# Second-layer attention scores: three bf16 terms in three passes, or two float32r terms in one

## The chip, the cores and the metric

The kernel runs on one core of one Trainium2 chip, in one launch. The metric is the device time of that launch in microseconds. A profiled execution of the same program gives a span and the instructions of each engine: PE (TensorE matmul), PEld (its weight loads), ACT (ScalarE), DVE (VectorE), POOL (GpSimd) and SP (SyncE, which issues most DMAs).

## What is computed

The input x has shape (4, 64, 64, 128): four images of 4096 tokens with 128 channels. Layer 0 is a gated residual block with two 3x3 convolutions and masked single-head attention. Layer 1 is full attention with 16 heads of 8 channels, a gated feed-forward block, and a mixture of 8 experts of which each token uses two. The change concerns the attention of layer 1. Cut to that, the reference is

```python
q = (x @ wq).reshape(bsz, seqlen, N_HEADS, HEAD_DIM)
k = (x @ wk).reshape(bsz, seqlen, N_HEADS, HEAD_DIM)
v = (x @ wv).reshape(bsz, seqlen, N_HEADS, HEAD_DIM)
scores = jnp.einsum('bqhd,bkhd->bhqk', q, k)
probs = jax.nn.softmax(scores.astype(jnp.float32), axis=-1).astype(q.dtype)
attn = jnp.einsum('bhqk,bkhd->bqhd', probs, v).reshape(bsz, seqlen, DIM)
```

Everything is in float32. For each image and head this is a 4096 x 4096 matrix of scores, so 268 million exponentials per image and 1074 million in all.

## The kernel before

The four images (batches) are worked one after the other. For each, the program runs layer 0's convolutions (L245 to L307), layer 0's attention (L309 to L427), layer 1's attention (`l1_attention`, L430 to L564), the feed-forward block and the experts. A tile framework turns the program into one instruction stream per engine. It works out which instruction must wait for which from the tiles and slices that they read and write, and it may put an instruction of a later part between earlier ones when those are not ready.

**Exact scores from short numbers.** Queries and keys are float32. To multiply them on bf16 paths without loss, `three_terms` (L234) splits each number into three bf16 terms: ScalarE rounds the first, VectorE subtracts it, GpSimd rounds the second, VectorE subtracts again. This is done for 8 chunks of 512 tokens per image (L435 to L445), and the terms are stored in DRAM tensors `d_k` and `d_q`.

**Layout.** Four heads make a group (`NG1` = 4 groups), each in its own slot of 32 rows (partitions). `keys(g)` (L469) loads a group's keys: 8 channels x 3 key terms = 24 rows per head, all 4096 tokens, in bf16. Two buffers hold this group's keys and the next one's. `queries(g, c)` (L477) loads 512 queries with each of their three terms repeated over the three key terms. A score needs all nine products of terms; the 24 rows give the products of three key terms with one query term, and three matmuls that accumulate in PSUM add up the three query terms.

**Order of the work.** A block is one group with one chunk of 512 queries: 32 blocks per image, 128 in all. In each block the loop at L541 runs over 32 key tiles of 128 keys. One such step is

```python
            for kt in range(NT):
                ss = [s_tile(), s_tile()]
                for i in range(NTERM):
                    for j in range(NSLOT):
...
                late.append((n, kt, es))
                if len(late) > LAG:
                    finish(*late.pop(0))
```

that is, 12 score matmuls (L546) in three passes over four slots, into two PSUM tiles of 128 x 1024 (two heads each, two banks each), then two exponentials on ScalarE (L556) from PSUM to SBUF, then the value matmuls (`add_up`, L507 and L509) of the step two steps back (`LAG` = 2). Those are plain float32, one per head, each with its own 32 output columns of the array, and they accumulate values and row sums in `acc` over the block. There are three PSUM score tiles, so a score matmul must wait until the exponential three tiles back has read its tile. At a block's end VectorE copies `acc` to SBUF (L524); the next block's first value matmuls must wait for that. One step later, four transposes (L495) and two VectorE instructions (L498, L500) turn the block's result into rows by token.

SP's queue carries, in this order, the chunk stores (L444, L445), the loads of queries (L483, four per block, one block ahead) and the loads of keys (L474, four per group, a group ahead).

Of the kernel before, what the change touches and what calls it, by code (L numbers as in the profile page):

```python
# [8 lines left out]

FP = mybir.dt.float32  # L10
BF = mybir.dt.bfloat16
AF = mybir.ActivationFunctionType
ALU = mybir.AluOpType
AX = mybir.AxisListType

P = 128
C = 128
IMG = 64
N = IMG * IMG
NT = N // P  # L20
QB = 512
NQ = N // QB
# [4 lines left out]
SLOT = 32  # L27
NSLOT = P // SLOT
# [3 lines left out]
NH1, HD1 = 16, 8  # L32
NG1 = NH1 // NSLOT
HIDDEN = 344
FCH = [(0, 128), (128, 128), (256, 88)]
NE = 8

NTERM = 3  # L40
# [49 lines left out]
def fast_path(ctx: ExitStack, tc: tile.TileContext, a: dict, where: dict, out: bass.AP, verdict):  # L90

    nc = tc.nc
    x = a["x"]
    B = x.shape[0]
    LAG = 2

    const = ctx.enter_context(tc.tile_pool(name="f_const", bufs=1))
    big = ctx.enter_context(tc.tile_pool(name="f_big", bufs=1))
    ep = ctx.enter_context(tc.tile_pool(name="f_ep", bufs=8))
    wk = ctx.enter_context(tc.tile_pool(name="f_wk", bufs=2))  # L100
    sm = ctx.enter_context(tc.tile_pool(name="f_sm", bufs=2))
    dram = ctx.enter_context(tc.tile_pool(name="f_dram", bufs=2, space=bass.MemoryType.DRAM))
    ps_s = ctx.enter_context(tc.tile_pool(name="f_ps_s", bufs=3, space=bass.MemoryType.PSUM))
    ps_o = ctx.enter_context(tc.tile_pool(name="f_ps_o", bufs=1, space=bass.MemoryType.PSUM))
    ps_m = ctx.enter_context(tc.tile_pool(name="f_ps_m", bufs=1, space=bass.MemoryType.PSUM))

    def s_tile():
        return ps_s.tile([P, 1024], FP, tag="s", name="s")

    def m_tile():  # L110
        return ps_m.tile([P, QB], FP, tag="m", name="m")
# [1 line left out]
    def e_tile():  # L113
        return ep.tile([P, 1024], FP, tag="e", name="e")
# [119 lines left out]
    def three_terms(src):  # L234

        xs = wk.tile([P, NTERM, 1024], BF, tag="x", name="x")
        rest = e_tile()
        nc.scalar.copy(xs[:, 0, :], src)
        nc.vector.tensor_tensor(rest, src, xs[:, 0, :], ALU.subtract)
        nc.gpsimd.tensor_copy(xs[:, 1, :], rest)  # L240
        nc.vector.tensor_tensor(xs[:, 2, :], rest, xs[:, 1, :], ALU.subtract)
        return xs
# [186 lines left out]

    def l1_attention(b, yT, h):  # L430

        d_k = dram.tile([P, NTERM, N], BF, tag="k1", name="d_k1")
        d_q = dram.tile([NQ, P, NTERM, QB], BF, tag="q1", name="d_q1")
        top = sm.tile([P, 2, NQ], FP, tag="top", name="top")
        for c in range(NQ):  # L435
            cols = slice(c * QB, (c + 1) * QB)
            ps = s_tile()
            nc.tensor.matmul(ps[:, :QB], lhsT=wq1, rhs=yT[:, cols], start=True, stop=True)
            nc.tensor.matmul(ps[:, QB:], lhsT=wk1, rhs=yT[:, cols], start=True, stop=True)
            nc.vector.tensor_reduce(  # L440
                top[:, :, c], ps.rearrange("p (j n) -> p j n", j=2), AX.X, ALU.max, apply_absolute_value=True
            )
            terms = three_terms(ps)
            nc.sync.dma_start(out=d_k[:, :, cols], in_=terms[:, :, QB:])  # L444
            nc.sync.dma_start(out=d_q[c], in_=terms[:, :, :QB])  # L445

        tops = sm.tile([P, 2], FP, tag="tops", name="tops")
        nc.vector.tensor_reduce(tops, top, AX.X, ALU.max)
        nc.vector.tensor_tensor(seen[:, 2, b : b + 1], tops[:, 0:1], tops[:, 1:2], ALU.mult)
        nc.vector.tensor_scalar(seen[:, 2, b : b + 1], seen[:, 2, b : b + 1], 1e30, None, ALU.min)  # L450

        top_v = sm.tile([P, NT // 8], FP, tag="topv", name="topv")
        for s in range(NT // 8):
            ps = s_tile()
            for k in range(8):
                i = 8 * s + k
                nc.tensor.matmul(
                    ps[:, k * P : (k + 1) * P], lhsT=yT[:, i * P : (i + 1) * P], rhs=wv1, start=True, stop=True
                )
            nc.vector.tensor_copy(  # L460
                v1[:, 8 * s : 8 * s + 8, :, 1:], ps.rearrange("p (k h d) -> p k h d", h=NH1, d=HD1)
            )
            nc.vector.tensor_reduce(top_v[:, s : s + 1], ps, AX.X, ALU.max, apply_absolute_value=True)
        nc.vector.tensor_reduce(seen[:, 3, b : b + 1], top_v, AX.X, ALU.max)


        rows = HD1 * NTERM

        def keys(g):  # L469
            kx = big.tile([P, N], BF, tag="kx", bufs=2, name="kx")  # L470
            for j in range(NSLOT):
                head = NSLOT * g + j
                src = d_k[head * HD1 : (head + 1) * HD1].rearrange("d y n -> (d y) n")
                nc.sync.dma_start(out=kx[j * SLOT : j * SLOT + rows, :], in_=src)  # L474
            return kx

        def queries(g, c):  # L477

            qx = wk.tile([P, NTERM, QB], BF, tag="qx", name="qx")
            for j in range(NSLOT):  # L480
                head = NSLOT * g + j
                src = d_q[c][head * HD1 : (head + 1) * HD1].rearrange("d x n -> d (x n)")
                nc.sync.dma_start(  # L483
                    out=qx[j * SLOT : j * SLOT + rows].rearrange("p x n -> p (x n)"),
                    in_=src.unsqueeze(1).to_broadcast([HD1, NTERM, NTERM * QB]),
                )
            return qx

        nt = big.tile([P, NT, C], FP, tag="y", name="nt")

        def by_token(g, c, at):

            ps = m_tile()
            for k in range(4):
                nc.tensor.transpose(ps[:, k * P : (k + 1) * P], at[:, k * P : (k + 1) * P], ident)  # L495
            pj = ps.rearrange("p (k j s) -> p k j s", j=NSLOT, s=SLOT)
            rc = sm.tile([P, 4, NSLOT], FP, tag="rc", name="rc")
            nc.vector.reciprocal(rc, pj[:, :, :, 0])  # L498
            gc = slice(g * NSLOT * HD1, (g + 1) * NSLOT * HD1)
            nc.vector.tensor_tensor(  # L500
                nt[:, 4 * c : 4 * c + 4, gc].rearrange("p k (j d) -> p k j d", d=HD1),
                pj[:, :, :, 1 : 1 + HD1],
                rc.unsqueeze(3).to_broadcast([P, 4, NSLOT, HD1]),
                ALU.mult,
            )

        def add_up(g, c, kt, es):  # L507
            for j in range(NSLOT):
                nc.tensor.matmul(  # L509
                    acc[j * SLOT : j * SLOT + 1 + HD1, :],  # L510
                    lhsT=v1[:, kt, NSLOT * g + j, :],
                    rhs=es[j // 2][:, (j % 2) * QB : (j % 2 + 1) * QB],
                    start=kt == 0,
                    stop=kt == NT - 1,
                )

        order = [(g, c) for g in range(NG1) for c in range(NQ)]
        ready = []

        def finish(n, kt, es):  # L520
            add_up(*order[n], kt, es)
            if kt == NT - 1:
                at = wk.tile([P, QB], FP, tag="at", name="at1")
                nc.vector.tensor_copy(at, acc)  # L524
                ready.append(at)
            if kt == 1 and ready:
                by_token(*order[n - 1], ready.pop())

        kx, qx = keys(0), queries(0, 0)
        kx_next = qx_next = None  # L530
        late = []
        for n, (g, c) in enumerate(order):
            if n:
                qx = qx_next
                if c == 0:
                    kx = kx_next
            if n + 1 < len(order):
                qx_next = queries(*order[n + 1])
            if c == 0 and g + 1 < NG1:
                kx_next = keys(g + 1)  # L540
            for kt in range(NT):  # L541
                ss = [s_tile(), s_tile()]
                for i in range(NTERM):
                    for j in range(NSLOT):
                        r = slice(j * SLOT, j * SLOT + rows)
                        nc.tensor.matmul(  # L546
                            ss[j // 2][:, (j % 2) * QB : (j % 2 + 1) * QB],
                            lhsT=kx[r, kt * P : (kt + 1) * P],
                            rhs=qx[r, i, :],
                            start=i == 0,  # L550
                            stop=i == NTERM - 1,
                        )
                es = []
                for ps in ss:
                    e = e_tile()
                    nc.scalar.activation(e, ps, AF.Exp)  # L556
                    es.append(e)
                late.append((n, kt, es))
                if len(late) > LAG:
                    finish(*late.pop(0))  # L560
        for item in late:
            finish(*item)
        by_token(*order[-1], ready.pop())
        return nt  # L564

# [847 lines left out]
```

## Time and profile before

| what | value |
|---|---|
| time, median of 3 runs | 10427.56 us (10423.74 to 10437.85) |
| time of the profiled execution | 10433.93 us |
| its span | 10432.1 us |
| mean granted TensorE clock | 0.966 |
| exponentials of layer 1 (L556) | 8192 |
| score matmuls (L546) | 49,152 records, median 374 ns |
| value matmuls (L509) | 32,768 records, median 597 ns |
| first and last exponential of layer 1's attention, image 0 | starts 419.6 us, next image's starts 3023.0 us |

A busy time is the time in which at least one instruction of an engine was under way. Matmuls overlap: a record of 374 ns does not mean that the next one starts 374 ns later. So a busy PE is not a PE at its peak, and the same holds for ACT, whose instructions overlap by about a tenth. To see what paces a loop one needs the distance from start to start, and what an engine was waiting for in the gaps. A profile row of a group gives line, engine, operation, output and inputs, shapes and count; then busy time and mean length of one (ns), and after the bar the idle time before them with what ended it.

### The profile page before, as it was taken

Reading aid. Unit: us, or ns where it says so; the run is one execution under the profiler, and the core shown is the slowest. Engines: PE = TensorE matmul, PEld = TensorE weight load, DVE = VectorE, ACT = ScalarE, POOL = GpSimd, SP = SyncE. Lnnn points to the kernel's source line nnn. Section 1 sums busy time; section 2 is a strip of 40 time slices with the busy share of each in tenths; the row PEclk is TensorE's granted clock in tenths of the full one; section 3 lists DMA queues with packets and bytes.
Section 4 is the critical chain, followed back from the end, with each engine's and each line's share of the span. In section 5 each row is a group of like instructions: output and inputs, shape, how many; then the busy total and the mean of one; then the engine's idle time right before and its main releaser. Section 6 shows DMA issues by size and latency. Waiting matters only on the chain.

```text
span 10432.1 us, 204188 instructions
## 1 busy us (share of the span) xinstructions
PE 9972.6 (96%) x90561; PEld 3179.9 (30%) x90565; DVE 1150.2 (11%) x3539; ACT 8198.4 (79%) x8965; POOL 184.3 (2%) x177
## 2 busy tenths in 40 slices
PE   8899999997989999999798999999979899999997
PEld 4322222224432222222442222222244222222224
DVE  1200000004220000000412000000051200000005
ACT  1699999991169999999116999999911799999991
POOL 0000000000000000000000000000000000000000
PEclk9999999998999999999889999999988999999998
DMA  1100000000010000000001000000000100000000
GB/s 26 35 6 10 6 9 7 6 5 15 5 34 6 10 6 9 7 6 5 16 4 35 7 9 6 10 6 6 5 16 4 35 7 9 6 10 6 6 5 9
DMA packets 86914, 112.51 MB, mean 11 GB/s; under 512 B 8835, under 2 KB 71779, under 8 KB 84195
## 3 DMA queue, kind: packets, MB, share of 16 engines
q1 hardware_dynamic: 83267, 97.59, 3.2%
q8 instruction: 710, 11.63, 0.5%
q10 hardware_dynamic: 2752, 1.77, 0.1%
q14 instruction: 185, 1.52, 0.0%
HBM read 64.99 MB, written 34.34 MB: 10 GB/s over the span
## 4 chain that ended last, share of the span: by engine, by line
PE 93%; DVE 4%; DMA 1%; ACT 1%; issue 0%; SPq 0%; POOL 0%; DVEq 0%; ACTq 0%; POOLq 0%
PE acc L509 38%; PE s L546 35%; PE s L291 5%; PE s L276 2%; PE s L666 2%; PE acc L381 2%; DVE t L675 2%; PE s L402 1%; PE s L583 1%; PE s L584 1%; PE m L495 1%; PE m L592 1%; PE m L231 1%; PE s L367 1%; PE m L574 0%
## 5 line engine op out<-in xcount | busy, mean ns | idle before, releaser
L556 ACT ACTIVATE e<-s 128x1024 f32<-128x1024 f32 x8192 | 7642.7, 1022 | 149.5 <-PE s L546 149.5
L509 PE MATMUL acc<-e,f_v 128*9 128x512 f32 x32768 | 4296.2, 595 | 4.5 <-ACT e L556 4.5
L546 PE MATMUL s<-qx,kx 24*128 24x512 bf16 x49152 | 3926.0, 377 | 29.5 <-DMA kx<-d_k 28.5
L546 PEld LDWEIGHTS <-kx 24*128 24x128 bf16 x49152 | 1548.0, 91 | 3823.5 <-issue 3467.2
L509 PEld LDWEIGHTS acc<-e,f_v 128*9 128x9 f32 x32768 | 486.7, 88 | 1753.4 <-issue 1687.1
L524 DVE COPY at<-acc 128x512 f32<-128x512 f32 x128 | 88.6, 692 | 7149.6 <-PE acc L509 7149.6
L291 PE MATMUL s<-c,f_w2c 128*128 128x512 f32 x1152 | 499.9, 592 | 0.0
L666 PE MATMUL s<-f_we,e 128*128 128x512 f32 x512 | 313.1, 763 | 58.2 <-DVE t L675 53.2
L299 ACT ACTIVATE e<-s,f_b 128x512 f32<-128x512 f32 x32 | 22.0, 687 | 422.8 <-PE s L291 422.7
L675 DVE SCALAR_TENSOR_TENSOR t<-s,gate,t 128x128 f32<-128x128 f32 x1024 | 305.9, 343 | 5.3 <-PE s L666 2.5
L291 PEld LDWEIGHTS s<-c,f_w2c 128*128 128x128 f32 x1152 | 215.5, 189 | 263.5 <-issue 263.5
L418 ACT ACTIVATE e<-s 128x1024 f32<-128x1024 f32 x224 | 217.6, 1021 | 91.1 <-PE s L402 90.4
L276 PE MATMUL s<-e,f_w1c 128*128 128x512 f32 x576 | 249.9, 596 | 3.1 <-DVE t L675 1.9
L402 PE MATMUL s<-qk 36*128 36x512 bf16 (+1 forms) x576 | 169.3, 388 | 76.0 <-DMA qk<-d_q 74.1
L655 ACT COPY g<-m 8x512 f32<-8x512 f32 x32 | 18.4, 575 | 230.4 <-PE m L653 230.4
L232 ACT COPY e<-m 128x512 f32<-128x512 f32 x64 | 37.5, 586 | 204.4 <-PE m L231 204.4
L381 PE MATMUL acc<-e,f_v 128*17 128x512 f32 (+3 forms) x1152 | 197.7, 600 | 0.0
L586 ACT ACTIVATE e<-s 128x512 f32<-128x512 f32 (+1 forms) x96 | 56.8, 596 | 165.6 <-PE s L584 165.5
L588 POOL TENSOR_TENSOR t<-t,h 128x512 f32<-128x512 f32 x32 | 40.5, 1266 | 8117.7 <-DVE h L577 8117.7
L666 PEld LDWEIGHTS s<-f_we,e 128*128 128x128 f32 x512 | 118.7, 247 | 202.9 <-issue 120.9
L283 ACT ACTIVATE c<-s,f_b 128x1024 f32<-128x1024 f32 x16 | 17.9, 1118 | 186.7 <-PE s L276 186.7
L276 PEld LDWEIGHTS s<-e,f_w1c 128*128 128x128 f32 x576 | 109.2, 190 | 141.7 <-issue 141.0
(146 smaller groups left out, 2962.0 us busy)
## 6 DMA issues: line engine op xcount, KB each, us to landing
qx<-d_q SPq DMA_DIRECT2D x512, 72.0 KB
d_k<-x SPq DMA_DIRECT2D x32, 384.0 KB
d_q<-x SPq DMA_DIRECT2D x32, 384.0 KB
kx<-d_k SPq DMA_DIRECT2D x64, 192.0 KB
t<-in_x_dram SPq DMA_DIRECT2D x16, 512.0 KB
out_dram<-t SPq DMA_DIRECT2D x32, 256.0 KB
f_w2c<-in_L_conv_W_dram ACTq DMA_DIRECT2D x1, 1152.0 KB
qk<-d_q SPq DMA_DIRECT2D x12, 96.0 KB
```

The costliest lines, as they stand in the source:

```text
L231: nc.tensor.transpose(ps[:, k * P : (k + 1) * P], src[:, k, :], ident)
L276: nc.tensor.matmul(rows(ps[:, h * QB : (h + 1) * QB]), lhsT=w1c[:, tap, :], rhs=e0[:, r0 : r0 + 8, kx : kx + IMG], start=(tap == 0), stop= ...
L291: nc.tensor.matmul(rows(ps[:, h * QB : (h + 1) * QB]), lhsT=w2c[:, tap, h * C : (h + 1) * C], rhs=c1[:, 8 * c + ky : 8 * c + ky + 8, kx : ...
L367: nc.tensor.matmul(ps[:, k * C : (k + 1) * C], lhsT=l_, rhs=w3f, start=True, stop=True)
L381: nc.tensor.matmul(acc[j * SLOT : j * SLOT + 1 + DV0, off:], lhsT=v0[:, kt, :], rhs=e[:, lo:hi], start=r == 0, stop=r == c,)
L402: nc.tensor.matmul(ps[:, lo:hi], lhsT=kx[:kr, kt * P : (kt + 1) * P], rhs=qx[:kr, c * QB + off : (c + 1) * QB], start=True, stop=r < c,)
L418: nc.scalar.activation(e, ps, AF.Exp)
L509: nc.tensor.matmul(acc[j * SLOT : j * SLOT + 1 + HD1, :], lhsT=v1[:, kt, NSLOT * g + j, :], rhs=es[j // 2][:, (j % 2) * QB : (j % 2 + 1) * ...
L546: nc.tensor.matmul(ss[j // 2][:, (j % 2) * QB : (j % 2 + 1) * QB], lhsT=kx[r, kt * P : (kt + 1) * P], rhs=qx[r, i, :], start=i == 0, stop= ...
L556: nc.scalar.activation(e, ps, AF.Exp)
L666: nc.tensor.matmul(px[:, h * QB : (h + 1) * QB], lhsT=yT[:, k * P : (k + 1) * P], rhs=we_f[:, h * QB : (h + 1) * QB], start=True, stop=True,)
L675: nc.vector.scalar_tensor_tensor(tk, px[:, n * C : (n + 1) * C], gate[:, k, n : n + 1], tk, ALU.mult, ALU.add)
```

## The change

Queries and keys of layer 1 are split into two terms of the type float32r (a rounded form of float32) instead of three of bf16. ScalarE writes the rounded first term, VectorE the remainder; GpSimd and the second subtraction are no longer used here. The terms take 4 bytes each. All four products of terms fit into a head's slot (8 channels x 2 x 2 = 32 rows), so one matmul per head replaces three. The queries are stored twice in DRAM, in the layout in which they are loaded, so a block's queries are one load. The keys have one buffer instead of two; a group's keys are loaded in four quarters of 1024 tokens, after the last scores of the group before. The three PSUM score tiles become slices of one tile of six banks. The loop runs over tiles of two heads; `LAG` = 2 counts such tiles, so the value matmuls of a step come after the scores of the next step. What L524 and L495 do is unchanged.

```diff
-            terms = three_terms(ps)
+            terms = wk.tile([P, 2, 1024], FP, tag="x", name="two")
+            nc.scalar.copy(terms[:, 0, :].bitcast(FR), ps)
+            nc.vector.tensor_tensor(terms[:, 1, :].bitcast(FR), ps, terms[:, 0, :], ALU.subtract)
             nc.sync.dma_start(out=d_k[:, :, cols], in_=terms[:, :, QB:])
-            nc.sync.dma_start(out=d_q[c], in_=terms[:, :, :QB])
+            for y in range(2):
+                nc.sync.dma_start(out=d_q[c][:, y], in_=terms[:, :, :QB])
...
+        kx = big.tile([P, N], FP, tag="kx", bufs=1, name="kx")
         def keys(g):
-            kx = big.tile([P, N], BF, tag="kx", bufs=2, name="kx")
-            for j in range(NSLOT):
...
+            src = d_k[g * SLOT : (g + 1) * SLOT].rearrange("d y n -> (d y) n")
+            for s in range(4):
+                cols = slice(s * N // 4, (s + 1) * N // 4)
+                nc.sync.dma_start(
+                    out=kx[:, cols], in_=src[:, cols].unsqueeze(1).to_broadcast([2 * SLOT, 2, N // 4])
+                )
...
+        work = [(n, kt, j) for n in range(len(order)) for kt in range(NT) for j in range(NSLOT)]
...
+        for first in range(0, len(work), WIDE):
+            now = work[first : first + WIDE]
+            ps = s_tile(WIDE)
+            for i, (n, kt, j) in enumerate(now):
...
+                r = slice(j * SLOT, (j + 1) * SLOT)
+                nc.tensor.matmul(
+                    ps[:, i * QB : (i + 1) * QB],
+                    lhsT=kx[r, kt * P : (kt + 1) * P].bitcast(FR),
+                    rhs=qx[r, :].bitcast(FR),
+                    start=True,
+                    stop=True,
+                )
+                g, c = order[n]
+                if c == NQ - 1 and kt == NT - 1 and j == NSLOT - 1 and g + 1 < NG1:
+                    keys(g + 1)
+            e = ep.tile([P, WIDE * QB], FP, tag="e", name="e")
+            nc.scalar.activation(e[:, : len(now) * QB], ps[:, : len(now) * QB], AF.Exp)
+            late.append([(w, e[:, i * QB : (i + 1) * QB]) for i, w in enumerate(now)])
+            if len(late) > LAG:
+                late_now = late.pop(0)
...
+            for (n, kt, j), part in late_now:
+                have[j] = part
+                if j == NSLOT - 1:
+                    add_up(n, kt, have)
```

More of the change, by code (lines that the diff above doesn't have):

```diff
@@ L11 @@
 BF = mybir.dt.bfloat16
+FR = mybir.dt.float32r
 AF = mybir.ActivationFunctionType
@@ L95, in fast_path @@
     LAG = 2
+    WIDE = 2
     const = ctx.enter_context(tc.tile_pool(name="f_const", bufs=1))
@@ L102, in fast_path, with s_tile @@
     dram = ctx.enter_context(tc.tile_pool(name="f_dram", bufs=2, space=bass.MemoryType.DRAM))
-    ps_s = ctx.enter_context(tc.tile_pool(name="f_ps_s", bufs=3, space=bass.MemoryType.PSUM))
+    ps_s = ctx.enter_context(tc.tile_pool(name="f_ps_s", bufs=1, space=bass.MemoryType.PSUM))
     ps_o = ctx.enter_context(tc.tile_pool(name="f_ps_o", bufs=1, space=bass.MemoryType.PSUM))
     ps_m = ctx.enter_context(tc.tile_pool(name="f_ps_m", bufs=1, space=bass.MemoryType.PSUM))
-    def s_tile():
-        return ps_s.tile([P, 1024], FP, tag="s", name="s")
+    banks = ps_s.tile([P, 6, QB], FP, tag="s", name="s")
+    turn = [0]
+    def s_tile(n=2):
+        at = turn[0] if turn[0] + n <= 6 else 0
+        turn[0] = at + n
+        return banks[:, at : at + n, :].rearrange("p b n -> p (b n)")
     def m_tile():
@@ L430, in l1_attention @@
     def l1_attention(b, yT, h):
-        d_k = dram.tile([P, NTERM, N], BF, tag="k1", name="d_k1")
-        d_q = dram.tile([NQ, P, NTERM, QB], BF, tag="q1", name="d_q1")
+        d_k = dram.tile([P, 2, N], FP, tag="k1", name="d_k1")
+        d_q = dram.tile([NQ, P, 2, 2, QB], FP, tag="q1", name="d_q1")
         top = sm.tile([P, 2, NQ], FP, tag="top", name="top")
@@ L464, in l1_attention @@
         nc.vector.tensor_reduce(seen[:, 3, b : b + 1], top_v, AX.X, ALU.max)
-        rows = HD1 * NTERM
+        kx = big.tile([P, N], FP, tag="kx", bufs=1, name="kx")
         def keys(g):
-            kx = big.tile([P, N], BF, tag="kx", bufs=2, name="kx")
-            for j in range(NSLOT):
[L472 to L475, printed above, removed]
-        def queries(g, c):
[L479 to L486, printed above, removed]
+            src = d_k[g * SLOT : (g + 1) * SLOT].rearrange("d y n -> (d y) n")
[4 more added lines that the diff above has]
+                )
+        def queries(g, c):
+            qx = wk.tile([P, QB], FP, tag="qx", name="qx")
+            nc.sync.dma_start(out=qx, in_=d_q[c][g * SLOT : (g + 1) * SLOT].rearrange("d y x n -> (d y x) n"))
             return qx
@@ L505, in by_token, with add_up @@
             )
-        def add_up(g, c, kt, es):
+        order = [(g, c) for g in range(NG1) for c in range(NQ)]
+        ready = []
+        def add_up(n, kt, es):
+            g, c = order[n]
             for j in range(NSLOT):
@@ L511, in add_up @@
                     lhsT=v1[:, kt, NSLOT * g + j, :],
-                    rhs=es[j // 2][:, (j % 2) * QB : (j % 2 + 1) * QB],
+                    rhs=es[j],
                     start=kt == 0,
@@ L515, in add_up @@
                 )
[L517 to L521, printed above, removed]
             if kt == NT - 1:
@@ L527, in finish @@
                 by_token(*order[n - 1], ready.pop())
[L529 to L560, printed above, removed]
@@ L561, in l1_attention @@
-        for item in late:
-            finish(*item)
+        work = [(n, kt, j) for n in range(len(order)) for kt in range(NT) for j in range(NSLOT)]
+        late, qx, qx_next = [], None, queries(0, 0)
+        have = {}
+        keys(0)
+        for first in range(0, len(work), WIDE):
+            now = work[first : first + WIDE]
+            ps = s_tile(WIDE)
+            for i, (n, kt, j) in enumerate(now):
+                if kt == 0 and j == 0:
+                    qx = qx_next
+                    if n + 1 < len(order):
+                        qx_next = queries(*order[n + 1])
+                r = slice(j * SLOT, (j + 1) * SLOT)
[6 more added lines that the diff above has]
+                )
+                g, c = order[n]
+                if c == NQ - 1 and kt == NT - 1 and j == NSLOT - 1 and g + 1 < NG1:
[5 more added lines that the diff above has]
+                late_now = late.pop(0)
+            else:
+                late_now = []
+            if first + WIDE >= len(work):
+                late_now += [w for ws in late for w in ws]
+            for (n, kt, j), part in late_now:
+                have[j] = part
+                if j == NSLOT - 1:
+                    add_up(n, kt, have)
```

## The prediction, made before the result was known

> **What bounds the kernel now.** I read the page's busy shares first, then its costliest groups.
>
> ```profile
> PE 9972.6 (96%) x90561; PEld 3179.9 (30%) x90565; DVE 1150.2 (11%) x3539; ACT 8198.4 (79%) x8965; POOL 184.3 (2%) x177
> ...
> PE 93%; DVE 4%; DMA 1%; ACT 1%; issue 0%; SPq 0%; POOL 0%; DVEq 0%; ACTq 0%; POOLq 0%
> ...
> L556 ACT ACTIVATE e<-s 128x1024 f32<-128x1024 f32 x8192 | 7642.7, 1022 | 149.5 <-PE s L546 149.5
> L509 PE MATMUL acc<-e,f_v 128*9 128x512 f32 x32768 | 4296.2, 595 | 4.5 <-ACT e L556 4.5
> L546 PE MATMUL s<-qx,kx 24*128 24x512 bf16 x49152 | 3926.0, 377 | 29.5 <-DMA kx<-d_k 28.5
> ```
>
> The chain that ended last gives PE 93%, which reads as "PE-bound, so a third of the score matmuls is worth 2/3 of 3926 us". The L556 row forbids that: in the same stretch ACT is busy 7642.7 us and waited for PE only 149.5 us. The two engines run nose to tail. The timeline of a piece of second-layer attention shows how (start, length, engine, line, count):
>
> ```profile
> 698.56 7.56 ACT L556 ACTIVATE e<-s 128x1024 f32<-128x1024 f32 x8
> ...
> 700.39 1.04 PE L509 MATMUL acc<-e,f_v 128*9 128x512 f32 x8
> ...
> 701.37 0.99 PE L546 MATMUL s<-qx,kx 24*128 24x512 bf16 x12
> ```
>
> A step (one key tile, four heads) is 12 score matmuls, 8 records of value matmuls and two exponentials. Eight exponentials in 7.56 us start (7.56-1.02)/7 = 0.934 us apart. The question is how much of that is ACT's own pace. The next lines are ACT alone over two blocks (a block is 32 steps), then the same place over 1.9 us, then PE there:
>
> ```profile
> 1035.65 59.70 ACT L556 ACTIVATE e<-s 128x1024 f32<-128x1024 f32 x64 [0.51 <-PE s L546]
> 1095.87 59.70 ACT L556 ACTIVATE e<-s 128x1024 f32<-128x1024 f32 x64 [0.51 <-PE s L546]
> ```
> ```profile
> 1035.65 2.85 ACT L556 ACTIVATE e<-s 128x1024 f32<-128x1024 f32 x3 [0.51 <-PE s L546]
> ```
> ```profile
> 1031.30 0.12 PEld L509 LDWEIGHTS acc<-e,f_v 128*9 128x9 f32 x8 [0.46 <-DVE at L524]
> ...
> 1033.17 1.05 PE L509 MATMUL acc<-e,f_v 128*9 128x512 f32 x8
> ...
> 1034.14 0.65 PE L495 MATMUL m<-f_consts,at 128*128 128x128 f32 x4
> ...
> 1034.73 0.83 PE L546 MATMUL s<-qx,kx 24*128 24x512 bf16 x12
> ...
> 1035.49 1.05 PE L509 MATMUL acc<-e,f_v 128*9 128x512 f32 x8
> ```
>
> Right after a stall, where scores lie ready, three exponentials start (2.85-1.02)/2 = 0.915 us apart; 0.92 is common elsewhere. I take 0.917 as ACT's floor. A block now lasts 1095.87-1035.65 = 60.22 us. At the floor it would last 64 x 0.917 = 58.69. So of 60.22, only 1.53 us can be won while 64 exponentials remain: 0.9 from steps in which ACT waits a little, 0.6 from one stall of 0.51 us behind the four transposes of L495 (value matmuls to scores take 1034.73-1033.17 = 1.56 there, 0.98 elsewhere). **ACT is the bound that the change cannot move**: 8192 exponentials of 1024 columns stay.
>
> **The change, part by part.**
>
> *Scores.* Per step, 12 bf16 matmuls in three accumulating passes become 4 float32r matmuls in one. Before, three passes without a wait take 1035.49-1034.73 = 0.75 us until the value matmuls; a pass is (0.83-0.37)/2 = 0.23 (0.37 is one matmul's record), so one pass leaves 0.75-0.46 = 0.29. PE's step is then 0.98+0.29 = 1.27 us of ACT's 1.83: PE ceases to pace. No row shows float32r. Lower bound: the bf16 pass, 0.23. Upper bound: plain fp32, where the chain lists 36 records of L291 (18 matmuls) in 15.46 us, 0.86 each, 0.63 more than bf16. I take the bf16 end: L509's 16,384 calls make 32,768 records, so fp32 runs as two records each, which a number already rounded to the short type has no need of. Weight loads: 91 ns now, 140 (L495) to 189 (L291) for 128 f32 columns; 0 to 0.1 us more per step.
>
> The Trainium skill, "TensorE: Matmul & The Clock Gate", section "Weight-path perf modes", says fast weight load never applies to fp32, which speaks against 4-byte keys; the loads above agree in direction, and since they fit the slack worked out below, the sum would be the same with the rule or without it.
>
> *Order.* LAG counts tiles of two heads now, so values follow scores by one step, not two. This ties a loop over two steps: exponential 1.02, hop to PE 0.06 (the copy at L524 to 1031.30), values 0.98, score 0.39, hop to ACT 0.09 (1034.73+0.83 to 1035.65), next exponential's turn 0.92: 3.46 us against 2 x 1.834 = 3.67. Slack 0.21 us: ACT stays the pace, but not by much. Two passes (0.23 more) would use it up; weight loads would not. At a block's end the copy of acc (0.69) delays the next values by hundredths only, since these now wait for an exponential anyway; that wait hides it. The transposes cost 0.58 in that loop, less 0.21 slack: 0.37 stays. Block: 58.69+0.37 = 59.06; 60.22-59.06 = 1.16; x128 blocks = **-148 us** (at best 64 x 0.915 and no stall: -212; with two passes (3.46+0.23)/2 = 1.845 a step, block 59.6: -77; worse is rival 1).
>
> *PSUM.* Three tiles become slices of one tile of six banks. If waits were by whole tile, each score would wait for the exponential before it. This trace shows waits by bank, in layer 0, where two heads share a tile:
>
> ```profile
> 280.69 0.23 PE L402 MATMUL s<-qk 36*128 36x128 bf16 x1
> ...
> 280.80 0.66 ACT L415 ACTIVATE e<-s 128x384 f32<-128x384 f32 x2 [0.89 <-PE s L412]
> ```
>
> The second bank's matmul starts at 280.69, before the first bank is read at 280.80, though it stands after it in the code. Cost 0.
>
> *Keys in one buffer.* Twelve times a group's keys are reloaded in quarters of 512 KB. A quarter is free when its eight key tiles are done in the group's last block; the first is then due 24 steps (44 us) later, the last also 24 steps into the next block. Loads land some 3 us after issue (413.8 to 416.9 at the start of a batch). They stand on SP behind the next block's queries; behind them wait only queries that are not due before the block after. Hidden, 0. If the cover is gone: 12 x 3 to 9 us = +36 to +110.
>
> *Splitting and storing.* The window (length, busy times of the engines, granted clock, DMA share, GB/s) and the group are of batch 0's chunks and of all chunks' ScalarE casts. Per chunk (8 per batch) a GpSimd cast (1.04) and a DVE subtraction (1.22) leave the chain from scores to store, one SP issue (0.6) joins, and bytes double, 768 to 1536 KB.
>
> ```profile
> 388.00:400.00 12.00, 6.44 (x24) 3.59 (x23) 9.64 (x10) 2.52 (x3) 2.74 (x3) 0.92 0.62 211
> ```
> ```profile
> L238 ACT CAST x<-s 128x1024 bf16<-128x1024 f32 x32 | 32.4, 1012 | 104.4 <-DMA d_q<-x 69.1 <-DVE top L440 25.7 <-PE s L457 3.9
> ```
>
> In this window DMA moves 211 GB/s at 0.62 share, so 340 at most: a chunk needs 1.573 MB/340 = 4.6 us against the 4.9 us per chunk at which L444 issues now (386.4 to 411.0 for five). ACT already waits 69.1 us for these stores. So shorter chain and longer transfer nearly cancel: -10 to +15 us per batch (no tail at all; 1573/211 = 7.5 us a chunk for six chunks). Against that, the first scores need only a quarter of the keys (two chunks), not all eight: about 5 of the 8 us between the last store (411.5) and the first exponential (419.7) go. I take -5 per batch, **-20 us**. The first 14 us after it run at clock 0.50, where ACT starts only 7 exponentials; PE's shorter step lets a few more through, I take -1.5 per batch (**-6**).
>
> Sum: -148-20-6 = -174. The profiled execution took 10433.9 us (span 10432.1 and 1.8 around it): 10260. It lies 6.4 above the median of 10427.6, so I forecast 10253.
>
> **Rivals.**
> 1. *float32r costs like fp32, or its row groups don't run side by side (slower).* Place: PE in each of 4096 steps. It decides once a step's four products take 0.27 us more until they are ready (2 x 1.864-3.46, where 1.864 = (60.22-0.58)/32) or occupy PE 0.58 us longer. Four passes: (3.46+0.63)/2 = 2.05 per step, block 32 x 2.05+0.58 = 66.2, +5.9 x 128 = +760, about 11165. One after another: 0.98+0.29+3 x 0.23 = 1.96, block 63.3, +394, about 10800. For it: no row of this type. Against: bf16 row groups and fp32 column groups both overlap here (8 value records in 1.05 us, 0.6 each).
> 2. *The win shrinks:* keys or stores are exposed after all, or ACT keeps 0.934 a piece. Then 148 becomes 30 to 70: 10330 to 10400.
> 3. *Clock.* PE is idle for part of each step now. Rows from the feed-forward stage (window, length, busy time of PE first; the last three columns are granted clock, DMA share, GB/s):
>
> ```profile
> 2401.70:2405.10 3.40, 2.44 (x19) 2.06 (x18) 0.68 (x1) 0.59 (x1) 0.00 (x0) 1.00 0.00 0
> 2405.10:2408.50 3.40, 1.82 (x14) 1.39 (x13) 1.18 (x3) 0.59 (x1) 0.00 (x0) 1.00 0.00 0
> 2408.50:2411.90 3.40, 2.58 (x12) 1.89 (x10) 0.69 (x1) 0.00 (x0) 1.13 (x1) 0.51 0.00 0
> ```
>
> PE busy 2.44 of 3.40 (72%) is followed by full clock, 1.82 (54%) by half. After the change a step has 1.04+0.4 of 1.83 busy, 79%: full clock. At half clock a step would take 2 x 1.27 = 2.5 us, +0.7 x 4096 = +2900 if throughout. The same skill page, section "HAM oscillation", asks only for no idle gap over about 3.4 us; these rows fell to half clock with 1.6 us idle in all, so the measurement rules, and by the page the price would be nil.
> 4. *Waits by whole tile after all:* a tile costs 1.02+0.06+0.39+0.09 = 1.56 instead of 0.94, +5000 us.
>
> **How the numbers follow.** Likeliest 0.68, 10253 (own range 10190 to 10330); rival 2 0.10; a win that vanishes within 0.2% (21 us, about what a measurement can tell) 0.05; rival 1 0.13; rivals 3 and 4 0.02 each. Faster 0.78, same 0.05, slower 0.17. The range takes in the first two cases, 10185 to 10410, and leaves out the slow ones.
>
> **What would show it.** Exponentials 0.915 to 0.92 us apart with no PE wait but one of about 0.4 us per block; PE busy near 80% with clock 1.00; score records a third of 49,152 or fewer; no idle time put down to kx. Wrong if score records last near 0.6 us or come in pairs, if their four starts lie 0.2 us apart, or if ACT's idle time before L556 grows.

## The result, and the profile after

The changed kernel takes 17839.39 us (median; 17826.88 to 17855.25) where the kernel before takes 10426.43 (10423.74 to 10437.85) beside it: a ratio of 1.711, with an interval of 1.708 to 1.714. The forecast of 10253 was wrong by its sign. What happened is the rival that had been given 2 in 100: waits by whole tile.

The page after: busy shares, the chain that ended last by engine, and the costliest groups.

```profile
PE 14903.7 (83%) x57793; PEld 3610.4 (20%) x57797; DVE 1181.7 (7%) x3507; ACT 8957.8 (50%) x8965; POOL 150.0 (1%) x145
...
ACT 48%; PE 40%; issue 6%; DVE 4%; ACTq 1%; another core or an unknown queue 1%; DMA 0%; SPq 0%; POOL 0%; DVEq 0%; POOLq 0%
...
L557 ACT ACTIVATE e<-s 128x1024 f32<-128x1024 f32 x8192 | 8381.3, 1023 | 5625.1 <-PE s L546 5625.1
L519 PE MATMUL acc<-e,f_v 128*9 128x512 f32 x32768 | 8471.0, 595 | 0.8 <-ACT e L557 0.8
L546 PE MATMUL s<-qx,kx 32*128 32x512 f32 x16384 | 4102.5, 495 | 1745.2 <-ACT e L557 1735.4
```

The score matmuls are a third in number (16,384 for 49,152), and no exponential became longer (1023 ns against 1022). But the chain, 93% PE before, now changes hands: ACT 48%, PE 40%. The exponentials waited 5625.1 us for scores (149.5 before), and the scores waited 1735.4 us for exponentials. Two engines that wait for each other this long look like a ring with too few buffers. The list of waits (engine and line, what it waited for, us in total, times, longest) gives the count:

```profile
PEld s L546 <- ACT e L557: 9125.9, 8064, 1.7
ACT e L557 <- PE s L546: 5625.1, 8192, 24.6
```

All 8192 exponentials waited for scores, and 8064 pairs of scores for an exponential (8192 less 128, the number of blocks). With three free buffers one side may have to wait, but not both in every tile: in the kernel before, 144 exponentials waited for scores. The timeline of second-layer attention shows one turn of the ring:

```profile
1100.88 1.02 ACT L557 ACTIVATE e<-s 128x1024 f32<-128x1024 f32 x1 [0.65 <-PE s L546]
1101.96 0.50 PE L546 MATMUL s<-qx,kx 32*128 32x512 f32 x2 [0.21 <-ACT e L557]
...
1102.38 1.03 PE L519 MATMUL acc<-e,f_v 128*9 128x512 f32 x4
1102.56 1.02 ACT L557 ACTIVATE e<-s 128x1024 f32<-128x1024 f32 x1 [0.65 <-PE s L546]
```

The exponential ends at 1101.90; 0.06 later the next scores start; 0.60 after that the next exponential. 1.02+0.06+0.60 = 1.68 us per tile, where the kernel before needed 0.94. The two engines take turns, though four of the six banks stand idle. (PE's 83% is no sign of a PE at its limit: in the 60 us from 1100 it is busy 51.85, and still waits in every tile.)

Where the 7421 us between the two spans (17853.4 and 10432.1) lie, by the first and the last exponential of each image:

| | before | after | difference |
|---|---|---|---|
| attention of layer 1, first start to last end, per image | 1933 | 3477 | 4 x 1544 = 6176 |
| from there to the next image's first | 665 to 671 | 971 to 988 | about 3 x 311 |
| before the first image's, and after the last's | 419.6 and 273.9 | 584.5 and 421.8 | 165 and 148 |

A sixth of the loss, 1245 us, is outside the loop that was rewritten: convolutions, layer 0's attention, feed-forward and experts draw their PSUM from the same `s_tile`. The granted clock was 1.00 in the 60 us from 1100.

### The profile page after: what moved, and what is told of

The parts are those of the page before. It is cut to its first block, busy times and chain, and to the rows that moved or that the text cites. A ratio compares the mean times of both kernels' runs of the same rounds, so it can differ in the third digit from the quotient of the medians.

```text
span 17853.4 us, 138310 instructions
## 1 busy us (share of the span) xinstructions
PE 14903.7 (83%) x57793; PEld 3610.4 (20%) x57797; DVE 1181.7 (7%) x3507; ACT 8957.8 (50%) x8965; POOL 150.0 (1%) x145
## 4 chain that ended last, share of the span: by engine, by line
ACT 48%; PE 40%; issue 6%; DVE 4%; ACTq 1%; another core or an unknown queue 1%; DMA 0%; SPq 0%; POOL 0%; DVEq 0%; POOLq 0%
ACT e L557 46%; PE s L546 24%; PE s L301 3%; PE s L672 3%; PE acc L391 2%; PE acc L519 2%; DVE t L681 1%; PE s L286 1%; PE s L412 1%; ACTq L557 1%; PE s L589 1%; ACT e L428 1%; PE m L241 1%; PE m L501 1%
## 5 line engine op out<-in xcount | busy, mean ns | idle before, releaser
L557 ACT ACTIVATE e<-s 128x1024 f32<-128x1024 f32 x8192 | 8381.3, 1023 | 5625.1 <-PE s L546 5625.1
L519 PE MATMUL acc<-e,f_v 128*9 128x512 f32 x32768 | 8471.0, 595 | 0.8 <-ACT e L557 0.8
L546 PE MATMUL s<-qx,kx 32*128 32x512 f32 x16384 | 4102.5, 495 | 1745.2 <-ACT e L557 1735.4
L546 PEld LDWEIGHTS s<-qx,kx 32*128 32x128 f32 x16384 | 1513.1, 181 | 9157.2 <-ACT e L557 9125.9
L519 PEld LDWEIGHTS acc<-e,f_v 128*9 128x9 f32 x32768 | 864.3, 88 | 2017.3 <-issue 2012.8
L672 PE MATMUL s<-f_we,e 128*128 128x512 f32 x512 | 463.7, 1059 | 298.3 <-DVE t L681 298.3
L391 PE MATMUL acc<-e,f_v 128*17 128x512 f32 (+3 forms) x1152 | 450.7, 771 | 0.0
L428 ACT ACTIVATE e<-s 128x1024 f32<-128x1024 f32 x224 | 229.3, 1023 | 359.5 <-PE s L412 306.4
L589 PE MATMUL s<-e,f_fw 128*128 128x512 f32 (+1 forms) x192 | 127.7, 752 | 111.1 <-DVE gT L593 87.7
L501 PE MATMUL m<-f_consts,at 128*128 128x128 f32 x512 | 111.2, 300 | 101.7 <-DVE at L528 101.7
L448 PE MATMUL s<-yT,f_wq 128*128 128x512 f32 x64 | 65.6, 1128 | 107.3 <-DVE two L455 100.5
```

What stands on the lines that cost most here:

```text
L391: nc.tensor.matmul(acc[j * SLOT : j * SLOT + 1 + DV0, off:], lhsT=v0[:, kt, :], rhs=e[:, lo:hi], start=r == 0, stop=r == c,)
L519: nc.tensor.matmul(acc[j * SLOT : j * SLOT + 1 + HD1, :], lhsT=v1[:, kt, NSLOT * g + j, :], rhs=es[j], start=kt == 0, stop=kt == NT - 1,)
L546: nc.tensor.matmul(ps[:, i * QB : (i + 1) * QB], lhsT=kx[r, kt * P : (kt + 1) * P].bitcast(FR), rhs=qx[r, :].bitcast(FR), start=True, stop ...
L557: nc.scalar.activation(e[:, : len(now) * QB], ps[:, : len(now) * QB], AF.Exp)
L589: nc.tensor.matmul(ps[:size, :QB], lhsT=fw1[:, lo : lo + size], rhs=hT, start=True, stop=True)
L672: nc.tensor.matmul(px[:, h * QB : (h + 1) * QB], lhsT=yT[:, k * P : (k + 1) * P], rhs=we_f[:, h * QB : (h + 1) * QB], start=True, stop=True,)
```

## The experiments

The theory after the result: where scores and exponentials share a PSUM tile, the program's waits name that tile, not the banks of it that an instruction touches. (The description of the kernel before says that the framework works waits out from tiles and slices; for this tile the theory denies the slices.) Six banks as one tile are one buffer, so each score pair waits for the exponential just before it. Rivals: the float32r matmuls, the single key buffer, or the lag of two tiles cost the time; or the view that `s_tile` returns (a rearranged one) hides the banks from a framework that would else see them.

### Three tiles again, all else as changed

```diff
-    ps_s = ctx.enter_context(tc.tile_pool(name="f_ps_s", bufs=1, space=bass.MemoryType.PSUM))
+    ps_s = ctx.enter_context(tc.tile_pool(name="f_ps_s", bufs=3, space=bass.MemoryType.PSUM))
-    banks = ps_s.tile([P, 6, QB], FP, tag="s", name="s")
-    turn = [0]
...
-        return banks[:, at : at + n, :].rearrange("p b n -> p (b n)")
+        return ps_s.tile([P, n * QB], FP, tag="s", name="s")
```

> The changed kernel with one thing undone: three PSUM score tiles of 128x1024 again, in place of slices of one tile of six banks. Theory A (the loss is the wait by whole tile: in the changed kernel each pair of score matmuls starts 0.05 us after the exponential just before it has ended, a tile takes 1.68 us): the waits go, a tile takes 0.917 to 0.92 us and the time is what the prediction forecast, 10253 us (10190 to 10330). Theory B (the float32r matmuls, their weight loads of 181 ns, or the values coming one step earlier make the loss): the time stays above 11000 us, with ACT waiting for the scores in most steps.

Measured: 10258.7 us (10231.02 to 10282.54), a ratio of 0.983 (0.981 to 0.985) to the kernel before. The page's groups, then a step in the timeline:

```profile
L551 ACT ACTIVATE e<-s 128x1024 f32<-128x1024 f32 x8192 | 7523.3, 1120 | 111.5 <-PE s L540 111.5
...
L540 PE MATMUL s<-qx,kx 32*128 32x512 f32 x16384 | 2111.5, 496 | 35.5 <-issue 32.7
```
```profile
1101.26 0.51 PE L540 MATMUL s<-qx,kx 32*128 32x512 f32 x4
1101.69 1.47 PE L513 MATMUL acc<-e,f_v 128*9 128x512 f32 x8
...
1103.09 0.51 PE L540 MATMUL s<-qx,kx 32*128 32x512 f32 x4
```

The exponentials' wait falls from 5625.1 to 111.5 us, the scores' wait for exponentials from 1735.4 to 2.7, and no wait for kx is listed. A step takes 1103.09-1101.26 = 1.83 us, two exponentials at 0.917. So the split, the keys and the lag together are a gain of 1.7%, and the one tile is the whole loss. The rivals that blame the other parts are out.

### The kernel before with one tile, and the changed kernel with a plain slice

```diff
-        return ps_s.tile([P, 1024], FP, tag="s", name="s")
+    banks = ps_s.tile([P, 6, QB], FP, tag="s", name="s")
...
+        return banks[:, at : at + n, :].rearrange("p b n -> p (b n)")
```

> The kernel before with only the PSUM tiles changed: six banks in one tile, slices handed out in turn; bf16 terms, three passes and order as before. Theory A: in the second layer a step becomes serial, hop 0.05, three passes 0.92, hop 0.09, two exponentials 0.92+1.02, about 3.0 us for 1.88, so +4600 us there, and the parts outside that attention lose what they lost in the changed kernel (some 310 us per image between the attentions, 1250 us in all): about 16300 us (15300 to 17300). Theory B: no change beyond 1%, 10430 us.

Measured: 16285.86 us, a ratio of 1.562 (1.558 to 1.565). bf16 scores and two key buffers, and the same disease. The timeline of one step:

```profile
1100.06 0.83 PE L552 MATMUL s<-qx,kx 24*128 24x512 bf16 x12
...
1100.99 1.94 ACT L562 ACTIVATE e<-s 128x1024 f32<-128x1024 f32 x2 [1.04 <-PE s L552]
1102.07 0.11 PEld L515 LDWEIGHTS acc<-e,f_v 128*9 128x9 f32 x4 [1.15 <-ACT e L562]
```

Its loop writes both tiles of a step before it reads them, so two exponentials share one wait (4096 waits, one per step). That fits its smaller loss: attention takes 3086 us per image, in the changed kernel 3477. Between images 966 to 986 us pass, as in the changed kernel: the loss outside the loop belongs to the tile as well.

The other run takes the rearrangement away and leaves the one tile.

```diff
-    banks = ps_s.tile([P, 6, QB], FP, tag="s", name="s")
+    banks = ps_s.tile([P, 6 * QB], FP, tag="s", name="s")
-        return banks[:, at : at + n, :].rearrange("p b n -> p (b n)")
+        return banks[:, at * QB : (at + n) * QB]
```

> The changed kernel with its six banks as a flat tile of 128x3072 and plain slices of 1024 columns, no third dimension and no rearranged view. If the wait belongs to the tile as a whole, nothing changes: about 17840 us, scores 0.05 us after the end of the exponential just before. If it belongs to the rearranged view, in which the bank can no longer be told, the waits go and the time is that of three_tiles, 10259 us.

Measured: 17850.74 us in a single run, with the changed kernel's 8192 and 8064 waits. The form of the view does not matter; the six banks of this tile wait as one.

That is not so for every tile of this program. The keys `kx` are one tile too, in SBUF, and the changed kernel loads their quarters one by one. SP's queue at the end of the first group (start, then the time from the first to the last of the four):

```profile
1372.77 81.27 SPq L486 DMA_DIRECT2D kx<-d_k  x4
```

The first quarter is reloaded from 1372.77 on, while the scores of the group still read the other quarters until about 1454. So here the waits tell the slices of a tile apart. Why they do for `kx` and not for the banks of `s` stays open.

### The lag

With three tiles, values still follow scores by one step. `LAG` = 4 makes it two, as before the change.

```diff
-    LAG = 2
+    LAG = 4
```

> three_tiles with LAG = 4 tiles, so that the values follow the scores by two steps as in the kernel before. If the loop over two steps (3.46 us of work against 3.67) is as short of slack as the prediction has it, the only thing that this frees is the stall of about 0.37 us per block behind the four transposes: 47 us less than three_tiles, about 10205 us. If values one step behind already cost more (ACT waits in every step of three_tiles), the gain is larger, 100 us or more. If ACT sets the pace in both, no difference beyond 50 us.

> three_tiles_lag4 once more, as the yardstick of this call: 10220 us again, 0.980 of the kernel before, with the exponentials' ends 0.917 us apart nearly throughout.

Measured: 10220.19 us, ratio 0.980 (0.978 to 0.982), and when repeated 10233.74, ratio 0.980 (0.978 to 0.983). A block takes 58.67 us between exponentials' ends, which is 64 x 0.917: nothing of the PE is left in it, the transposes' stall neither. It beats both kernels, and no version below is clearly faster. It lies 0.2 to 0.3 points below lag 2, about what the intervals can tell apart. Its list of waits is worth a look beside that of the changed kernel:

```profile
PEld s L540 <- ACT e L551: 4355.2, 7906, 1.7
ACT e L551 <- PE s L540: 75.7, 28, 16.2
```

The scores still wait for an exponential in nearly every tile, since PE runs ahead and fills all three. But only 28 exponentials wait for scores. Waits on one side show which engine sets the pace; waits on both sides in every tile show the ring.

### Float32r's place

```diff
-                    lhsT=kx[r, kt * P : (kt + 1) * P].bitcast(FR),
-                    rhs=qx[r, :].bitcast(FR),
+                    lhsT=kx[r, kt * P : (kt + 1) * P],
+                    rhs=qx[r, :],
```

> three_tiles with the score matmuls in plain float32: the same terms, rows and loads, but no float32r type on the two operands. It prices the type. If float32r runs one pass and float32 four, a step takes 0.63 us more until the scores are ready, (3.46+0.63)/2 = 2.05 us for 1.84: about 11150 us (10900 to 11500). If float32r is no cheaper than float32, both kernels take the same time.

Measured: 11702.58 us, ratio 1.122 (1.120 to 1.125), beyond the expected range. The timeline, PE only:

```profile
1099.61 1.39 PE L540 MATMUL s<-qx,kx 32*128 32x512 f32 x8
...
1100.93 1.04 PE L513 MATMUL acc<-e,f_v 128*9 128x512 f32 x8
...
1101.90 1.14 PE L540 MATMUL s<-qx,kx 32*128 32x512 f32 x8
...
1102.98 1.04 PE L513 MATMUL acc<-e,f_v 128*9 128x512 f32 x8
```

A plain fp32 matmul leaves two records, so four make x8, and the group holds PE for 1.07 or, every second step, 1.32 us until the values; as float32r it is x4 and 0.43 (1101.69-1101.26 above). So the type does what the change counted on: one record per matmul and a group that is two and a half to three times shorter. The expectation had the pace from the loop through the exponential, (3.46+0.63)/2 = 2.05 us a step. But PE sets it: two steps of PE take 1.07+0.97+1.32+0.98 = 4.34 us, 2.17 a step, and PE is busy for all of the 60 us from 1100. PE's step had been sized too low on two counts: the group that the 0.63 comes on top of is 0.43 and not 0.29, and every second group is 0.25 longer. Why every second one is longer stays open.

### Keys in one load

```diff
-            for s in range(4):
-                cols = slice(s * N // 4, (s + 1) * N // 4)
...
+            nc.sync.dma_start(out=kx, in_=src.unsqueeze(1).to_broadcast([2 * SLOT, 2, N]))
```

> three_tiles with a group's keys loaded by one DMA of 4096 tokens in place of four quarters. The prediction priced the quarters at nothing and their loss at 3 to 9 us for each of 12 reloads. If quarters are what hides the reload, each group begins with a wait for the whole load (2.1 MB at 340 GB/s is 6.2 us, and about 2 us until it starts), +75 to +120 us: 10335 to 10380 us. If the reload was exposed in three_tiles already, or is hidden in both, no change.

Measured: 10375.75 us, ratio 0.995 (0.993 to 0.996) against 0.983. Attention takes 1918.5 us per image against 1893.1, and an image has three reloads: 25.4/3 = 8.5 us each. The quarters hide that in full, since kx shows in no wait with them.

### Wider exponentials

ACT being the floor, tiles of three heads (two tiles of 1536 columns) should amortise what an exponential costs besides its columns.

```diff
-    WIDE = 2
+    WIDE = 3
-    ps_s = ctx.enter_context(tc.tile_pool(name="f_ps_s", bufs=3, space=bass.MemoryType.PSUM))
+    ps_s = ctx.enter_context(tc.tile_pool(name="f_ps_s", bufs=2, space=bass.MemoryType.PSUM))
...
```

Not shown are the wider PSUM tile itself, and five SBUF buffers for the exponentials' results in place of eight.

> three_tiles with tiles of three banks: two PSUM tiles of 128x1536, exponentials of 1536 columns, 5 instead of 8 SBUF buffers for them; the other parts use 1024 columns of two tiles instead of three. If ACT paces the loop (64 exponentials of 1024 columns take 58.75 us in three_tiles_lag4, 0.918 each, of which 1024 columns at 0.83 ns, from 1.02 less 0.60 us for 1024 and 512 columns, are 0.85), a third fewer instructions save 2731 x 0.066 = 180 us of ACT time: 10040 us, plus whatever the other parts lose with two tiles. If PE or the wait for tiles paces it with only two tiles in turn, no gain or a loss: 10250 us or more.

> wide3 with the values three tiles behind the scores instead of two. If wide3 still waits for PE behind the transposes or in steps that hold two groups of value matmuls, this gives some of it back, 40 us or more less than wide3. If ACT paces both, no difference beyond 25 us.

Measured: 10559.89 us, ratio 1.011 (1.008 to 1.013), and with lag 3 10545.61, 1.012 (1.010 to 1.013). The theory fell, and so did the lag as the reason. PE's lines:

```profile
1100.08 1.03 PE L513 MATMUL acc<-e,f_v 128*9 128x512 f32 x2
...
1101.04 0.50 PE L540 MATMUL s<-qx,kx 32*128 32x512 f32 x3
...
1101.48 1.04 PE L513 MATMUL acc<-e,f_v 128*9 128x512 f32 x6
...
1102.44 0.50 PE L540 MATMUL s<-qx,kx 32*128 32x512 f32 x3
```

Three heads per tile break a part of the value groups of four into groups of one (x2) and three (x6), and each holds PE as long as four: 1101.04-1100.08 = 0.96 for one head, 1102.44-1101.48 = 0.96 for three. So every tile now has a group of values, where three tiles in four would do. With 0.43 for scores a tile takes 1.40 us, more than the 1.34 that lie between the ends of such exponentials at their closest. PE became the pace again.

That is half of the loss. Attention takes 1926 us per image against 1893 with three tiles, 133 us in all; the first exponential starts at 464.1 us instead of 422.9, and 696 to 711 us pass between images instead of 664 to 673, together some 145 us. There the other parts have two PSUM tiles instead of three; a run that separates this was not made.

### The stretch between the layers

From layer 0 to the first exponential of layer 1 the prediction had counted -5 us per image. Three runs, each against lag 4: one more store per chunk; each quarter of the first keys loaded as soon as its two chunks are stored; and the first queries early as well.

```diff
-            for y in range(2):
+            for y in (0, 1, 1):
```
```diff
+            if c % 2:
+                keys(0, [c // 2])
```
```diff
+            if c == 0:
+                qx_first = queries(0, 0)
```

> three_tiles_lag4 with the second copy of the queries stored twice (0.524 MB more per chunk, 32 chunks, to the same place). It prices the stores. If the chunks wait for DMA bandwidth (its share is 0.97 to 0.99 there, 369 GB/s), each chunk takes 0.524/369 = 1.4 us longer, 8 x 1.4 = 11 us per image, +45 us: 10265 us. If the chunks are paced by the chain of casts and subtractions, or the stores are hidden, no difference beyond 15 us.

> three_tiles_lag4 with the first group's keys loaded quarter by quarter between the chunk stores (after every second chunk) instead of behind the last store. The prediction counted 5 us per image because the first scores need one quarter only; in three_tiles that gain is missing, and the four key loads stand behind all stores on SP. If their place is why, the first exponential comes 3 to 8 us sooner per image: 10190 to 10210 us. If the loads only take the bandwidth from the stores, which are the bound there, no gain, 10220 us.

> lag4_keys_early with the first block's queries loaded after the first chunk's stores too. In lag4_keys_early the first scores of image 0 waited 11.57 us for those queries, whose load stands on SP behind the last quarter of the keys (412.3), while PE was done at 406.3 and the last PSUM tile was read at 409.7. If that place on SP is all that was left of the wait, the first exponential comes about 8 us sooner per image (410.5 in place of 418.7): 32 us, ratio 0.975 to 0.977, 10200 us beside a before of 10448. If something else ends last there (the stores of the last chunks, the PSUM tiles), the ratio stays at 0.978 to 0.980.

The extra store: 10253.18 us, ratio 0.981 (0.979 to 0.983) against 0.980; a loss of some 20 us by the medians, which the intervals do not separate. It does not price a store alone: SP's queue shows that the framework also moved quarters of the keys between the stores (379, 393 and 408 us). Keys early: 10230.85, 0.978 (0.976 to 0.980), no clear gain either. The timeline tells why: the first queries' load now stood on SP behind the last quarter of the keys, and the scores waited for it.

```profile
417.82 1.22 PE L542 MATMUL s<-qx,kx 32*128 32x512 f32 x6 [11.57 <-DMA qx<-d_q]
```

With both early the first exponential did come sooner, at 409.4 us against 414.1. Yet the run took 10279.2 us, ratio 0.985 (0.983 to 0.988): slower. Attention takes 1902.5 us per image, where it took 1881 to 1884, and nearly all of the difference is in the first two blocks (18 and 3 us longer in the first image; each later one 58.67 as before). PE there:

```profile
429.18 0.50 PE L544 MATMUL s<-qx,kx 32*128 32x512 f32 x2
429.61 1.03 PE L518 MATMUL acc<-e,f_v 128*9 128x512 f32 x2
430.57 0.50 PE L544 MATMUL s<-qx,kx 32*128 32x512 f32 x2
431.00 1.04 PE L518 MATMUL acc<-e,f_v 128*9 128x512 f32 x6
```

It is the case of the wide tiles over again: PE's instructions came in another order, values in groups of one and three, two groups of 0.96 us per step instead of one, and a tile takes 1.40 us. With the edit the framework put the instructions in another order; how it chooses stays open.

## Why the prediction was wrong

**The step that failed: "This trace shows waits by bank ... Cost 0".** It rested on two rows of layer 0. The second bank's matmul at 280.69 was said to start before the first bank is read at 280.80. The rows ahead of those two, in the timeline of the kernel before, say otherwise:

```profile
278.93 0.28 PE L402 MATMUL s<-qk 36*128 36x256 bf16 x1
279.03 0.87 ACT L415 ACTIVATE e<-s 128x512 f32<-128x512 f32 x2
...
280.26 0.33 PE L402 MATMUL s<-qk 36*128 36x384 bf16 x1
```

On the diagonal four key tiles have 512, 384, 256 and 128 columns, two to a PSUM tile. So the matmul of 256 columns is the first bank of the second tile. The exponentials at 279.03 (x2) read the first banks of both tiles; only then come 384 and 128, the second banks, and the exponentials at 280.80 read these. No second bank is written before its tile's first bank has been read; in the code the 384 columns even stand ahead of the 256. So these rows show nothing of waits by bank, and they fit waits by tile. The profile leaves buffer numbers out: two tiles both called s were taken for one. The widths told them apart, and the view was entered one row too late. A wait by name is seen where layer 0's attention begins. Before, with three tiles, its second matmul runs ahead of the first exponential; the second of the two fences is the same stretch after the change, with all banks in one tile:

```profile
250.67 0.60 PE L402 MATMUL s<-qk 36*128 36x512 bf16 x1 [0.47 <-issue]
...
252.11 1.08 ACT L415 ACTIVATE e<-s 128x512 f32<-128x512 f32 x2
```

```profile
285.40 0.58 PE L412 MATMUL s<-qk 36*128 36x512 bf16 x1 [25.01 <-DMA qk<-d_q]
...
287.89 0.60 ACT L425 ACTIVATE e<-s 128x512 f32<-128x512 f32 x1
288.54 0.58 PE L412 MATMUL s<-qk 36*128 36x512 bf16 x1 [2.56 <-ACT e L425]
```

The exponential ends at 288.49, and the second matmul starts 0.05 us later.

**Rival 4 had the mechanism and missed the size.** It gave 1.02+0.06+0.39+0.09 = 1.56 us per tile. The term that was off is 0.39+0.09 from scores to exponential: it measured 0.60, of which the two float32r matmuls take 0.50. And it counted the loop alone, +5000, where the loop costs 6176 and the other users of `s_tile` 1245.

**The other steps held, but for the -20 of splitting and storing,** as the run with three tiles shows:

- *ACT's floor of 0.917 us* is the median distance between exponentials' ends in the kernel before, with three tiles and at lag 4, where 64 x 0.917 is the whole block.
- *Scores.* One pass with one record per matmul, right. A weight load takes 181 ns where it took 91. The group leaves 0.43 us until the values, not 0.29. In the loop over two steps four float32r matmuls take 0.51 where 0.39 was put. That takes 0.12 of the 0.21 us of slack, so ACT stayed the pace; the transposes' stall is 0.47 us per block instead of 0.37. Attention fell by 4 x 39.8 = 159 us; -148 and -6 had been forecast.
- *Keys in one buffer:* hidden. Uncovered they cost 8.5 us each, near the top of "3 to 9".
- *Splitting and storing, -20:* it came to nothing. From the issue of the last store to the first exponential 9.8 us pass (413.1 to 422.9), where 8.1 passed before (411.5 to 419.6), and 664 to 673 us lie between images' attentions (665 to 671). The start alone says little: at lag 4, with the same stores, it is 413.3. The window's last columns are clock, DMA share and GB/s; the second line is SP's queue:

```profile
388.00:400.00 12.00, 6.78 (x12) 2.02 (x10) 7.18 (x8) 3.04 (x3) 0.00 (x0) 0.89 0.99 369
```
```profile
414.70 3.94 SPq L480 DMA_DIRECT2D kx<-d_k  x4
```

  The stores now fill the DMA engines (0.99 share, 369 GB/s, against 0.62 and 211), and the keys' loads are issued in the queue's order, behind the last store (413.12). The first scores need only a quarter of the keys, but in this order none of it starts earlier; the runs with early keys moved it, and the gain was not clear.
- *Clock:* 1.00 in the 60 us from 1100, with three tiles as well. Rival 3 did not come. PE was not idle for a fifth of a step either: with three tiles it is busy 59.64 of these 60 us, since half of a step's values wait for an exponential (3844 waits) and a step's values so last 1.47 us instead of 1.05.

With three tiles the forecast of 10253 stands against 10258.7 measured. That it is so near is in part luck: the -20 did not come, and the single runs go from 10231 to 10283. One step, priced at nothing on a misread row, was worth 7,600 us.

## What to carry to other kernels

Before several buffers are merged into one tile, look for a place in the trace where one tile's first part is read while its second is still being written, and prove by shapes or code that it is the same tile: names without buffer numbers do not. When two engines each wait for the other once per tile (8192 and 8064 waits here), count the buffers that the waits see, not those in memory. Whether slices of a tile count as buffers has to be seen for that very tile: those of `kx` did, those of `s` did not. And price the worst case of a step that "costs nothing": here it outweighed all the rest of the change some forty times, which called for a chance above 2 in 100.

## What the runs showed of the hardware

- A group of fp32 value matmuls, each with its own 32 columns of the array, holds PE for 0.96 to 0.98 us with one head, three or four. Splitting a group doubles its cost.
- float32r: four matmuls of 32 rows in 0.43 us, one record each of 496 ns, against 1.07 to 1.32 us and two records each as plain fp32.
- The length of ACT's records is not its pace: in the kernel before the mean is 1022 ns, with three tiles 1120 and at lag 4 1375, while the ends are 0.917 us apart (median) in all three. A record can start before its predecessor has ended. Ends give the pace.
